# The last Mamba chunk of a convolution and attention network: one running sum in place of two, and the skip term on GpSimd

## The chip, the core and the metric

The kernel runs on one core of a Trainium2 chip. The metric is the device time of one execution in microseconds; of several runs the median is given. A core has five engines that run side by side, each with its own queue of instructions taken in order: TensorE (PE in the profile; its weight loads are the row PEld), VectorE (DVE), ScalarE (ACT), GpSimd (POOL) and SyncE (SP), which starts transfers. They meet through semaphores. TensorE writes its results into PSUM, from where VectorE and ScalarE read them; everything else lies in SBUF.

## What is computed

The network has four layers: a pair of Mamba blocks, a dynamic convolution, and two attention layers with mixtures of experts. The change concerns the second Mamba block of the first layer only:

```python
xs, res = jnp.split(u @ in_w + in_b, 2, axis=-1)
xs = silu(causal_conv(xs, conv_w) + conv_b)
dt, Bm, Cm = jnp.split(xs @ xproj_w, [DT_RANK, DT_RANK + D_STATE], axis=-1)
delta = softplus(dt @ dt_w + dt_b)
dA = exp(delta[..., None] * A)
dBu = delta[..., None] * Bm[:, :, None, :] * xs[..., None]
# scan over time: h = dA * h + dBu ; ys = sum over the 16 states of h * C
y = ys + xs * Dp
y = y * silu(res)
out = y @ out_w + out_b
# afterwards: x + layernorm(out)
```

There are 2 images of 1024 tokens, 256 channels, 512 inner channels and 16 states; all values are float32.

## The kernel before

A Mamba block (class `Mamba`) goes through its 2048 tokens in four chunks of 512 (`NCH`), and holds the inner channels as four groups of 128 partitions (`NDC`). A chunk has three parts. `front` makes xs, delta and du = delta times xs, and on GpSimd ends each of the four groups with the four operations of lines 405, 407, 409 and 411. `scan` runs over the 16 states n. For each of them GpSimd multiplies du by the broadcast row B in two halves of 128 x 1024 (line 461, tile `m_h`, six buffers), ScalarE makes exp(delta A) for each group (line 469, `m_da`), and VectorE runs the recurrence along the tokens (line 473). The states' outputs are then turned by TensorE so that tokens lie on partitions (line 440, `m_ht` in PSUM, three buffers), because C is then one number for each partition, and are multiplied by C and added to a running sum. This is the inner function `rest`, which is one state or more behind the recurrence. VectorE adds most of them into `ya` (line 449), but state 0 starts `ya` and state 10 (`ASIDE`) starts a second sum `yb`, each as an eviction by ScalarE (line 447).

`back` makes the gate: matmuls at line 496, evictions with bias at 500, Silu at 504. Then it turns both sums back to channels on partitions, and adds xs times D to them, all in one PSUM tile for each group. The skip is a product with a diagonal matrix (`skip`, line 517), and the sums are products with the identity (line 522). VectorE multiplies by the gate (526, in place of xs). Lines 534 and 538 form the output product, 545 the layer norm, 548 turns the result back, and for the last chunk 550 adds it into the residual `xt`, to which lines 510 to 513 have added the network's input and the norm's bias.

`layer0` strings this together as generators: while chunk u is scanned, `paced` advances the front of chunk u+1 and the back of chunk u-1 at given slots (first and end) of 63. In the last unit there is no next front. There `early()` runs in place of it, a part of the next layer's convolution for the first image (112 steps, line 795, tile `early_acc`), and the first seven steps of the chunk's own `back`: four gate groups, Silu, two residual additions. When the scan is over, `both` interleaves the rest of `back` with a last piece of that convolution, three convolution steps to one step of `back`. Then `layer1` begins. It loads the convolution's weights again (`pair`, line 773), turns the first image on POOL and PE (lines 889 and 890), and convolves the second image (line 795, tile `acc`), for which the last `xt` must be there.

The generators give the order in which the work is written. A scheduler decides the order in each engine's queue; an instruction can stand well before or after the slot at which it was written, but once the program is built, every queue is fixed. Tiles of one tag share buffers: the products of `back` and the gate use two PSUM buffers (tag `mm`).

Of the kernel before, what the change touches and what calls it, by code (L numbers as in the profile page):

```python
# [10 lines left out]
F32 = mybir.dt.float32  # L11
I32 = mybir.dt.int32
BF16 = mybir.dt.bfloat16
AF = mybir.ActivationFunctionType
# [5 lines left out]
P = 128  # L20
# [10 lines left out]
DI = 512  # L31
# [202 lines left out]
class Mamba:  # L234
# [177 lines left out]
            yield  # L412
        self.chunks[j] = xs, bd, ct, delta, du

    def scan(self, j, before, between, start=False):

        net, nc, m, scanp = self.net, self.net.nc, self.m, self.scanp
        xs, bd, ct, delta, du = self.chunks[j]
        state, first = self.state, self.first(j)
        ya = self.two.tile([P, TPC, DI], F32, tag="ya", name=f"{m}_ya_{j}")
        yb = self.one.tile([P, TPC, DI], F32, tag="yb", name=f"{m}_yb_{j}")
        self.chunks[j] = xs, ya, yb
        G = 2
        half = [P, G, TC]

        def keep(n, hs):  # L430
            for g, h in enumerate(hs):
                nc.scalar.copy(state[:, n, g * G : (g + 1) * G], h[:, :, TC - 1])

        def rest(n, hs):


            for i in range(TPC):
                ps = self.ps_ht.tile([P, DI], F32, tag="ht", name=f"{m}_ht_{j}_{n}_{i}")
                for dc in range(NDC):
                    nc.tensor.transpose(  # L440
                        ps[:, dc * P : (dc + 1) * P], hs[dc // G][:, dc % G, i * P : (i + 1) * P],
                        net.ident,
                    )
                yield
                c = ct[:, i, n : n + 1]
                if n in (0, self.ASIDE):
                    nc.scalar.activation((yb if n else ya)[:, i, :], ps, AF.Copy, scale=c)
                else:
                    nc.vector.scalar_tensor_tensor(  # L449
                        ya[:, i, :], ps, c, ya[:, i, :], ALU.mult, ALU.add  # L450
                    )
                if i == 0 and first:
                    keep(n, hs)

        for n in range(NS):
            b = scanp.tile([P, TC], F32, tag="b", name=f"{m}_b_{j}_{n}", bufs=4)
            nc.sync.dma_start(b, bd[n].partition_broadcast(P))
            hs = []
            for g in range(NDC // G):
                h = scanp.tile(half, F32, tag="h", name=f"{m}_h_{j}_{n}_{g}", bufs=6)  # L460
                made = (nc.vector if start and n == 0 else nc.gpsimd).tensor_mul(  # L461
                    h, du[:, g * G : (g + 1) * G, :], b.unsqueeze(1).to_broadcast(half)
                )
                hs.append(h)
            self.product = made
            for dc in range(NDC):
                da = self.ps_da.tile([P, TC], F32, tag="da", name=f"{m}_da_{j}_{n}_{dc}")
                i = dc * NS + n
                nc.scalar.activation(  # L469
                    da, delta[:, dc, :], AF.Exp, scale=self.aneg[:, i : i + 1]  # L470
                )
                h = hs[dc // G][:, dc % G, :]
                nc.vector.tensor_tensor_scan(  # L473
                    h, da, h, 0.0 if first else state[:, n, dc : dc + 1], ALU.mult, ALU.add
                )


                next(before, None)
                if n or dc:
                    next(between, None)  # L480
            before = chain(before, rest(n, hs))
        for _ in between:
            pass
        return before

    def back(self, j, last=False):


        net, nc, m, xt = self.net, self.net.nc, self.m, self.xt
        y, *sums = self.chunks.pop(j)  # L490
        tok = slice(j * TC, (j + 1) * TC)
        gate = self.one.tile([P, NDC, TC], F32, tag="gate", name=f"{m}_gate_{j}")
        for dc in range(NDC):
            ps = self.ps_mm.tile([P, TC], F32, tag="mm", name=f"{m}_g_{j}_{dc}")
            for kc in range(NCC):
                nc.tensor.matmul(  # L496
                    ps, lhsT=self.gate_sb[:, kc, dc * P : (dc + 1) * P], rhs=xt[:, kc, tok],
                    start=(kc == 0), stop=(kc == NCC - 1),
                )
            nc.scalar.activation(  # L500
                gate[:, dc, :], ps, AF.Identity, bias=net.col(f"{m}_in_b", NDC + dc)
            )
            yield
        nc.scalar.activation(gate, gate, AF.Silu)
        yield
        if last:
            for cc in range(NCC):
                x = self.one.tile([P, TC], F32, tag="r", name=f"{m}_x_{j}_{cc}", bufs=3)
                at = j % (HW // TC) * TC
                nc.sync.dma_start(x, self.x[j // (HW // TC), cc, :, at : at + TC])  # L510
                nc.gpsimd.tensor_scalar_add(x, x, net.col(f"{m}_ln_b", cc))
                nc.gpsimd.tensor_add(xt[:, cc, tok], xt[:, cc, tok], x)
                yield

        for dc in range(NDC):
            ps = self.ps_mm.tile([P, TC], F32, tag="mm", name=f"{m}_y_{j}_{dc}")
            nc.tensor.matmul(
                ps, lhsT=self.skip[:, dc, :], rhs=y[:, dc, :], start=True, stop=False
            )
            for k, ya in enumerate(sums):  # L520
                for i in range(TPC):
                    nc.tensor.matmul(
                        ps[:, i * P : (i + 1) * P], lhsT=ya[:, i, dc * P : (dc + 1) * P],
                        rhs=net.ident, start=False, stop=(k == 1 and i == TPC - 1),
                    )
            nc.vector.tensor_mul(y[:, dc, :], ps, gate[:, dc, :])
            yield
        o = self.one.tile([P, TPC, C], F32, tag="o", name=f"{m}_o_{j}")
        found = []
        for i in range(TPC):  # L530
            if i % 2 == 0:
                ps = self.ps_mm.tile([P, TC], F32, tag="mm", name=f"{m}_out_{j}_{i}")
            a = ps[:, i % 2 * C : (i % 2 + 1) * C]
            nc.tensor.matmul(
                a, lhsT=net.ones_row, rhs=self.out_b, start=True, stop=False
            )
            for dc in range(NDC):
                nc.tensor.matmul(
                    a, lhsT=y[:, dc, i * P : (i + 1) * P], rhs=self.out_sb[:, dc, :],
                    start=False, stop=(dc == NDC - 1),  # L540
                )
            found.append(a)
            yield
        tiles = [o[:, i, :] for i in range(TPC)]
        net.norm_rows(tiles, found, nc.scalar)
        yield
        for cc in range(NCC):
            ps = net.transposed(self.ps_mm, tiles, cc, "mm")
            if last:
                nc.vector.scalar_tensor_tensor(  # L550
                    xt[:, cc, tok], ps, net.col(f"{m}_ln_w", cc), xt[:, cc, tok],
                    ALU.mult, ALU.add,
                )
                yield
                continue
            r = self.one.tile([P, TC], F32, tag="r", name=f"{m}_r_{j}_{cc}", bufs=3)
            nc.scalar.activation(
                r, ps, AF.Identity, scale=net.col(f"{m}_ln_w", cc), bias=net.col(f"{m}_ln_b", cc)
            )
            nc.gpsimd.tensor_add(xt[:, cc, tok], xt[:, cc, tok], r)  # L560
            if self.x is not None:
                x = self.one.tile([P, TC], F32, tag="r", name=f"{m}_x_{j}_{cc}", bufs=3)
                at = j % (HW // TC) * TC
                nc.sync.dma_start(x, self.x[j // (HW // TC), cc, :, at : at + TC])
                nc.gpsimd.tensor_add(xt[:, cc, tok], xt[:, cc, tok], x)
            yield


def paced(n, parts):

    taken = [0] * len(parts)
    for slot in range(n):
        for i, (steps, many, first, end) in enumerate(parts):
            while taken[i] < many and slot >= first + (end - first) * taken[i] / many:
                next(steps, None)
                taken[i] += 1
        yield
    for steps, *_ in parts:
        for _ in steps:
            pass  # L580
# [11 lines left out]
def layer0(net, x, x_dram, m1, m2, load_image, taps, conv_dram, lg):  # L592
# [5 lines left out]
    with (  # L598
# [41 lines left out]
        for u, (m, j) in enumerate(units):  # L640
# [42 lines left out]
            own = m.back(j, u + 1 == len(units))  # L683
            if u + 1 == len(units):

                steps += [(islice(own, 7), 7, 44, 62)]
            before = m.scan(j, before, paced(63, steps), u == 0)
            done = [own]
        for _ in before:
            pass  # L690
# [1085 lines left out]
```

## Time and profile before

| what | us |
|---|---|
| three runs | 2169.64, 2165.42, 2167.72 |
| median | 2167.72 |
| profiled execution | 2167.17 |
| its span | 2165.4 |
| span up to the last chunk's first scan | 907 |
| from there to the first convolution matmul of layer 1 | 189 |
| from there to the end | 1069 |

| engine | busy us | share of the span |
|---|---|---|
| PE | 1890.4 | 87% |
| PEld | 1343.7 | 62% |
| DVE | 1403.3 | 65% |
| ACT | 957.8 | 44% |
| POOL | 1028.0 | 47% |

In the profile's lines a group reads: line of the kernel, engine, operation, tile written, tile read, partitions times elements, count. A note in brackets is the time for which the engine sat idle before that instruction, and what ended it. In the timeline the first number is the start in microseconds from the start of the span and the second the duration of the row. Rows of several instructions of one kind are merged (x8). The granted clock of TensorE is a share of full speed.

Around the last chunk the profile has these stages: the front of this chunk ends at about 904, the scan of its 16 states runs from 907 to 1048, the last addition into `ya` ends at 1061.5, the last convolution matmul of `early_acc` is at 1090, and `layer1`'s own convolution begins at 1096.4.

### The profile page before, as it was taken

To read this page: it belongs to the slowest core of one execution; us is meant where nothing else is said; L and a number is where in the kernel's file an instruction comes from. 1 tells how busy PE (TensorE), PEld (TensorE's weight loads), DVE (VectorE), ACT (ScalarE), POOL (GpSimd) and SP (SyncE) were. 2 spreads that over 40 slices of the span, in tenths; PEclk is the share of its full clock that TensorE was granted. 3 is DMA by queue.
4 is the path that set the end of the run, shared out by engine and by line. 5 is a ranking of instruction groups with operands and counts; after the bars stand their busy time and mean duration, and the time that the engine had idled before them with its cause. 6 is when DMAs were issued, how large, how long until landed. Compare 5 with 4: busy or idle time off the path is not lost.

```text
span 2165.4 us, 27316 instructions
## 1 busy us (share of the span) xinstructions
PE 1890.4 (87%) x9652; PEld 1343.7 (62%) x9652; DVE 1403.3 (65%) x2212; ACT 957.8 (44%) x1609; POOL 1028.0 (47%) x726
## 2 busy tenths in 40 slices
PE   6888899897989889799999899949999699859996
PEld 2364656555555555465655556639998467659994
DVE  6999999999999999897314575652222544432223
ACT  4677777767777767643213544311110132311011
POOL 3796788959697796964216410013332000023331
PEclk8969889798989979799999999969999799979997
DMA  3121121111112110310030100038998200069997
GB/s 107 45 69 40 37 65 41 59 33 54 54 48 61 38 51 31 87 38 25 10 55 1 49 15 10 20 121 299 328 327 305 83 10 10 20 221 325 331 327 286
DMA packets 90499, 223.87 MB, mean 103 GB/s; under 512 B 35467, under 2 KB 51728, under 8 KB 79732
## 3 DMA queue, kind: packets, MB, share of 16 engines
q1 hardware_dynamic: 77636, 198.29, 27.3%
q0 software_dynamic: 7728, 19.15, 2.9%
q10 hardware_dynamic: 4992, 4.59, 0.7%
q8 instruction: 81, 1.33, 0.3%
q14 instruction: 62, 0.51, 0.1%
HBM read 204.60 MB, written 19.37 MB: 103 GB/s over the span
## 4 chain that ended last, share of the span: by engine, by line
PE 30%; issue 17%; DVE 14%; POOL 10%; ACT 7%; DMA 4%; POOLq 0%; ACTq 0%; DVEq 0%
DVE m_h L473 7%; PE acc L795 3%; POOL x L1553 3%; POOL l_yd L1603 3%; DVE m_ya L449 3%; PE av L1309 3%; PE sc L1283 2%; DMA l_yd<-y,target 2%; PE early_acc L795 2%; PE h L1132 2%; PE m_ht L440 2%; ACT m_da L469 2%; POOL m_h L461 2%; PE w L1141 1%; DMA x<-l_zd,source 1%
## 5 line engine op out<-in xcount | busy, mean ns | idle before, releaser
L461 POOL TENSOR_TENSOR m_h<-m_du,m_b 128x1024 f32<-128x1024 f32 x254 | 594.4, 2363 | 223.4 <-PE m_ht L440 128.2
L440 PE MATMUL m_ht<-ident,m_h 128*128 128x128 f32 x2048 | 361.3, 308 | 105.3 <-DVE m_ya L449 76.2
L440 PEld LDWEIGHTS m_ht<-ident,m_h 128*128 128x128 f32 x2048 | 268.1, 157 | 297.2 <-issue 100.9
L469 ACT ACTIVATE m_da<-m_delta,m_aneg 128x512 f32<-128x512 f32 x512 | 348.9, 690 | 214.5 <-DVE m_h L473 214.0
L1553 POOL DMA_INDIRECT x<-l_zd,source x82 | 84.5, 1030 | 571.5 <-DVE source L1498 217.0
L449 DVE SCALAR_TENSOR_TENSOR m_ya<-m_ht,m_ct,m_ya 128x512 f32<-128x512 f32 x448 | 318.6, 731 | 31.1 <-PE m_ht L440 30.6
L473 DVE TENSOR_TENSOR_SCAN m_h<-m_da,m_state,m_h 128x512 f32<-128x512 f32 x256 | 316.8, 1267 | 29.2 <-POOL m_h L461 21.6
L473 DVE TENSOR_TENSOR_SCAN m_h<-m_da,m_h 128x512 f32<-128x512 f32 x256 | 302.7, 1207 | 18.0 <-ACT m_da L469 15.2
L1583 PEld LDWEIGHTS h<-xts,we 128*128 128x128 f32 x2528 | 297.4, 194 | 6.8 <-issue 3.1
L1583 PE MATMUL h<-xts,we 128*128 128x128 f32 x2528 | 298.5, 277 | 2.0 <-issue 1.5
L1590 DVE TENSOR_TENSOR hid<-hid,h 128x512 f32<-128x512 f32 x79 | 54.3, 687 | 256.1 <-PE h L1583 256.1
L1589 ACT ACTIVATE hid<-h 128x512 f32<-128x512 f32 x79 | 47.2, 597 | 381.6 <-PE h L1583 381.6
L1597 PE MATMUL o<-we,hid 128*128 128x256 f32 x632 | 150.4, 380 | 2.2 <-DVE y L1602 1.6
L1603 POOL DMA_INDIRECT l_yd<-y,target x79 | 79.0, 1000 | 142.6 <-DVE y L1602 137.9
L1597 PEld LDWEIGHTS o<-we,hid 128*128 128x128 f32 x632 | 113.7, 190 | 15.7 <-DVE y L1602 2.8
L336 PE MATMUL m_conv<-m_pre,m_taps 128*128 128x512 f32 x240 | 114.5, 596 | 6.1 <-ACT m_gate L500 5.6
L795 PE MATMUL early_acc<-x,early 128*98 128x448 f32 (+24 forms) x308 | 99.5, 449 | 0.0
L795 PE MATMUL acc<-x,pair 128*98 128x416 f32 (+21 forms) x308 | 94.1, 454 | 0.0
L1602 DVE COPY y<-o 128x256 f32<-128x256 f32 x79 | 33.5, 424 | 69.7 <-PE o L1597 69.7
L309 PE MATMUL m_in<-x,m_in_sb 128*128 128x512 f32 x128 | 67.3, 650 | 7.8 <-ACT m_pre L313 5.2
L496 PE MATMUL m_g<-x,m_gate_sb 128*128 128x512 f32 x128 | 69.9, 662 | 4.1 <-ACT m_o L168 2.1
L795 PEld LDWEIGHTS acc<-x,pair 128*98 128x98 f32 x308 | 48.0, 168 | 40.4 <-issue 35.0
(321 smaller groups left out, 2843.0 us busy)
## 6 DMA issues: line engine op xcount, KB each, us to landing
we<-in_l_experts_dram SPq DMA_DIRECT2D x82, 1536.0 KB, 9.4
m_b<-m_bd SPq DMA_DIRECT2D x128, 256.0 KB, 3.2
w<-in_l_w_dram SPq DMA_DIRECT2D x21, 256.0 KB, 3.9
l_zd<-l_z SPq DMA_DIRECT2D x7, 512.0 KB, 2.8
l_yl<-l_yd SPq DMA_DIRECT2D x10, 256.0 KB, 5.9
l_yl<-l_yd ACTq DMA_DIRECT2D x10, 256.0 KB, 5.9
early<-taps SPq DMA_DIRECT2D x7, 343.0 KB, 4.4
pair<-taps SPq DMA_DIRECT2D x7, 343.0 KB, 6.0
```

Of the source, the lines that this page charges most:

```text
L336: nc.tensor.matmul(ps, lhsT=self.taps[:, dc * 4 + k, :], rhs=pre[:, dc, k : k + TC], start=(k == 0), stop=(k == 3),)
L440: nc.tensor.transpose(ps[:, dc * P : (dc + 1) * P], hs[dc // G][:, dc % G, i * P : (i + 1) * P], net.ident,)
L449: nc.vector.scalar_tensor_tensor(ya[:, i, :], ps, c, ya[:, i, :], ALU.mult, ALU.add)
L461: made = (nc.vector if start and n == 0 else nc.gpsimd).tensor_mul(h, du[:, g * G : (g + 1) * G, :], b.unsqueeze(1).to_broadcast(half))
L469: nc.scalar.activation(da, delta[:, dc, :], AF.Exp, scale=self.aneg[:, i : i + 1])
L473: nc.vector.tensor_tensor_scan(h, da, h, 0.0 if first else state[:, n, dc : dc + 1], ALU.mult, ALU.add)
L496: nc.tensor.matmul(ps, lhsT=self.gate_sb[:, kc, dc * P : (dc + 1) * P], rhs=xt[:, kc, tok], start=(kc == 0), stop=(kc == NCC - 1),)
L795: nc.tensor.matmul(a[:, lo - 16 * k : hi - 16 * k, co : co + n], lhsT=lhsT, rhs=self.x[:, kc, b, lo - r0 : hi - r0, ci : ci + n], start=(u ...
L1553: nc.gpsimd.indirect_dma_start(out=x, out_offset=None, in_=zd[:, :], in_offset=bass.IndirectOffsetOnAxis(ap=source[:, g : g + 1], axis=0), ...
L1583: nc.tensor.matmul(ps[:, at], lhsT=w12[:, s, kc, at], rhs=xt[:, kc * P : (kc + 1) * P], start=(kc == 0), stop=(kc == NCC - 1),)
L1597: nc.tensor.matmul(ps[:, :C], lhsT=ht[:, mc * P : (mc + 1) * P], rhs=w[:, 8 + mc, :], start=(mc == 0), stop=(mc == NHC - 1),)
L1603: nc.gpsimd.indirect_dma_start(out=yd[g], out_offset=bass.IndirectOffsetOnAxis(ap=target[:, g : g + 1], axis=0), in_=y, in_offset=None, bo ...
```

## The change

For the last chunk alone there is no second sum: state 10 is added into `ya` by VectorE like the others. The skip is no longer a product of TensorE. GpSimd multiplies xs by D in place (four operations of 128 x 512, written for slots 6 to 40 of the scan), and after Silu multiplies this by the gate (four more, ahead of the residual additions). After the scan TensorE transposes `ya` only; VectorE multiplies the transpose by the gate and adds GpSimd's product, two operations for each group in place of one. The other chunks are as they were; the diagonal `skip` is still made for them.

```diff
-    def scan(self, j, before, between, start=False):
+    def scan(self, j, before, between, start=False, last=False):
...
-        yb = self.one.tile([P, TPC, DI], F32, tag="yb", name=f"{m}_yb_{j}")
-        self.chunks[j] = xs, ya, yb
+        sums = {0: ya}
+        if not last:
+            sums[self.ASIDE] = self.one.tile([P, TPC, DI], F32, tag="yb", name=f"{m}_yb_{j}")
+        self.chunks[j] = xs, *sums.values()
...
-                if n in (0, self.ASIDE):
-                    nc.scalar.activation((yb if n else ya)[:, i, :], ps, AF.Copy, scale=c)
+                if n in sums:
+                    nc.scalar.activation(sums[n][:, i, :], ps, AF.Copy, scale=c)
...
     def back(self, j, last=False):
...
+        if last:
+            for dc in range(NDC):
+                nc.gpsimd.tensor_scalar_mul(y[:, dc, :], y[:, dc, :], net.col(f"{m}_D", dc))
+                yield
         gate = self.one.tile([P, NDC, TC], F32, tag="gate", name=f"{m}_gate_{j}")
...
         nc.scalar.activation(gate, gate, AF.Silu)
         yield
         if last:
+            for dc in range(NDC):
+                nc.gpsimd.tensor_mul(y[:, dc, :], y[:, dc, :], gate[:, dc, :])
+                yield
...
             ps = self.ps_mm.tile([P, TC], F32, tag="mm", name=f"{m}_y_{j}_{dc}")
+            if last:
+                for i in range(TPC):
+                    nc.tensor.transpose(
+                        ps[:, i * P : (i + 1) * P], sums[0][:, i, dc * P : (dc + 1) * P], net.ident
+                    )
+                nc.vector.tensor_mul(gate[:, dc, :], ps, gate[:, dc, :])
+                nc.vector.tensor_add(y[:, dc, :], y[:, dc, :], gate[:, dc, :])
+                yield
+                continue
...
-                steps += [(islice(own, 7), 7, 44, 62)]
-            before = m.scan(j, before, paced(63, steps), u == 0)
+                steps += [(islice(own, 4), 4, 6, 40), (islice(own, 11), 11, 44, 62)]
+            before = m.scan(j, before, paced(63, steps), u == 0, u + 1 == len(units))
```

## The prediction

> **What bounds the kernel now.** I read the stretch in which the last chunk of Mamba is scanned and finished, 855 to 1100 us, because only that chunk's code changes. First the table by stage: which engine has no gap left.
>
> ```profile
> 905.00:920.00 15.00, 12.60 (x48) 6.73 (x47) 13.13 (x15) 7.56 (x14) 15.00 (x9) 0.83 0.51 120
> 920.00:935.00 15.00, 14.96 (x66) 8.87 (x67) 15.00 (x16) 8.47 (x13) 13.52 (x7) 1.00 0.27 67
> ...
> 1010.00:1025.00 15.00, 15.00 (x65) 9.32 (x64) 8.60 (x12) 6.32 (x8) 6.98 (x4) 1.00 0.00 0
> ...
> 1061.50:1071.00 9.50, 9.50 (x69) 7.92 (x67) 2.77 (x4) 0.00 (x0) 0.00 (x0) 1.00 0.01 2
> ```
>
> The columns are stretch, length, busy time of PE, PEld, DVE, ACT, POOL, then clock and DMA. The limit moves: GpSimd is full to 920, VectorE to about 964, TensorE from there to the end of the chunk (15.00 of 15, then 9.50 of 9.50). GpSimd looks half idle over the whole scan, but not where it begins. Second, the timeline of GpSimd there:
>
> ```profile
> 901.85 1.26 POOL L409 TENSOR_TENSOR m_delta<-m_delta,m_ln 128x512 f32<-128x512 f32 x1
> 903.19 1.26 POOL L411 TENSOR_TENSOR m_du<-m_delta,m_xs 128x512 f32<-128x512 f32 x1
> 904.41 4.66 POOL L461 TENSOR_TENSOR m_h<-m_du,m_b 128x1024 f32<-128x1024 f32 x2
> ...
> 916.24 16.25 POOL L461 TENSOR_TENSOR m_h<-m_du,m_b 128x1024 f32<-128x1024 f32 x7
> 933.96 4.67 POOL L461 TENSOR_TENSOR m_h<-m_du,m_b 128x1024 f32<-128x1024 f32 x2 [1.48 <-PE m_ht L440]
> ```
>
> From 855.75 to 932.5 no row has an idle note; the first one is at 933.96. Third, who waits for it, in the timeline of all engines:
>
> ```profile
> 903.14 0.69 ACT L500 ACTIVATE m_gate<-m_g,cols_sb 128x512 f32<-128x512 f32 x1 [6.55 <-POOL m_delta L409]
> ...
> 918.63 3.63 DVE L473 TENSOR_TENSOR_SCAN m_h<-m_da,m_state,m_h 128x512 f32<-128x512 f32 x3 [0.42 <-POOL m_h L461]
> ```
>
> VectorE waits for GpSimd's product at 918.63 and then has no pause over 0.1 us until 941.60. Fourth, the last two states of the scan, where TensorE is the limit:
>
> ```profile
> 1029.39 5.40 PE L496 MATMUL m_g<-x,m_gate_sb 128*128 128x512 f32 x8 [2.06 <-ACT m_o L168]
> ...
> 1039.71 4.68 POOL L461 TENSOR_TENSOR m_h<-m_du,m_b 128x1024 f32<-128x1024 f32 x2 [12.39 <-PE m_ht L440]
> ...
> 1045.13 1.27 DVE L473 TENSOR_TENSOR_SCAN m_h<-m_da,m_state,m_h 128x512 f32<-128x512 f32 x1
> ...
> 1046.32 0.72 DVE L449 SCALAR_TENSOR_TENSOR m_ya<-m_ht,m_ct,m_ya 128x512 f32<-128x512 f32 x1
> ...
> 1049.02 0.60 PE L440 MATMUL m_ht<-ident,m_h 128*128 128x128 f32 x4
> ```
>
> The two products of state 15 run back to back, and the second lies ready (1044.4) only 0.7 us before its scan at 1045.13. Fifth, the weight loads of TensorE in the tail, whose starts give its pace:
>
> ```profile
> 1063.67 0.97 PEld L522 LDWEIGHTS m_y<-ident,m_yb 128*128 128x128 f32 x8
> 1064.57 0.30 PEld L517 LDWEIGHTS m_y<-m_xs,m_skip 128*128 128x128 f32 x2
> 1065.11 0.19 PEld L522 LDWEIGHTS m_y<-ident,m_ya 128*128 128x128 f32 x1 [0.24 <-issue]
> ...
> 1066.32 0.97 PEld L522 LDWEIGHTS m_y<-ident,m_yb 128*128 128x128 f32 x8
> ...
> 1089.22 0.97 PEld L795 LDWEIGHTS early_acc<-x,early 128*98 128x98 f32 x10
> ```
>
> From one yb row to the next is 2.65 us for one quarter of y; the chain of waits has 0.86 of it for the skip and 1.78 for ya and yb together. Last, the price of the new GpSimd work, from single lines:
>
> ```profile
> L511 POOL TENSOR_SCALAR m_x<-m_x,cols_sb x2: 1562/1570/1578, 1047.5 to 1053.0; 128x512 f32<-128x512 f32 x2
> L409 POOL TENSOR_TENSOR m_delta<-m_delta,m_ln x28: 1262/1267/1282, 126.5 to 901.8; 128x512 f32<-128x512 f32 x28
> L409 DVE TENSOR_TENSOR m_delta<-m_delta,m_ln x4: 681/682/683, 43.8 to 50.1; 128x512 f32<-128x512 f32 x4
> ```
>
> **What the Trainium skill says.** GPSIMD Engine Reference, section 3.1 (Elementwise): a two-input operation takes about twice VectorE's time. The trace agrees: 1267 against 682 ns, 1.86 times. TensorE: Matmul & The Clock Gate, Part 1 (The HAM clock gate): after an idle window of about 3.4 us the array runs at half clock until a busy one has passed. The trace shows such a drop after a shorter pause: after the 2.06 us wait at 1029.39 eight matmuls took 5.40 us, where the pace of m_g at full clock (weight loads 0.43 apart from 1033.34) makes 3.44; 1.96 us were lost. Part 4 of that page (PE-mode transpose): transposes do not count as busy for that gate. No run here shows that alone.
>
> **The change part by part.** Besides durations I use the order in which the changed program holds each queue, which is fixed before it runs.
>
> 1. *y times D on GpSimd* (four tensor_scalar). Written for slots 6 to 40 of the scan, they nevertheless stand earlier: one behind each of the four L411 products of the last front, so three before the last L409 at 901.85 and the fourth before the first m_h of the last chunk at 904.41. That is the stretch without a gap. 4 x 1.57 = 6.3 us. Behind them wait the gate eviction on ScalarE (903.14, and with it the m_da behind it: +4.7) and all later m_h. State 0's products are ready 6.3 later, VectorE's scan at 918.63 starts at 924.9. From there it has no gap to take this up, and TensorE, which takes over as the limit at 964.14 out of a wait for VectorE's m_ya, begins its full stretch 6.3 later. Bounds: 4.7 if the fourth is hidden, 6.3 if all count. I take +6.3.
>
> 2. *State 10 added into ya by VectorE.* ScalarE loses four evictions of 0.68, and is not the limit (6.3 of 15 us busy). VectorE gains 4 x 0.73 = 2.9 us: one between the scans of state 12, three before those of state 13. Before 1012.78 VectorE stood idle 6.49 us waiting for m_h of state 13, which waits for the transposes of state 10; that hides all four. Cost 0; without that cover 2.9.
>
> 3. *y times gate on GpSimd* (four tensor_mul, 4 x 1.27 = 5.1 us). They stand between the two m_h of state 15. Silu ends at 1041.26, or 0.8 sooner since the last m_g moves ahead of an early-convolution matmul, so they wait for nothing: first product to 1042.05, gate products to 1047.1, second m_h to 1049.4, scan at 1049.45 in place of 1045.13. Behind that scan in VectorE's queue is the m_ya that started at 1046.32; it ends at 1051.4. It frees the PSUM buffer (three rotate) which m_ht at 1049.02 writes: TensorE waits until 1051.45, +2.4. That pause is longer than the one of 2.06, so I add its half-clock window, +1.9. Bounds: 0 (if the buffer is free) to 4.3. The eight x additions queued behind on GpSimd end near 1062 rather than 1055.95; L550 needs them only after 1080. On SP one residual load moves ahead of another; same cover.
>
> 4. *The tail.* Per quarter the four transposes that remain go at 0.11 each (rows of m_ht, eleven loads in 1.23), 0.44 in place of 2.65: 4 x 2.2 = 8.8 us less for TensorE. VectorE gets a second operation of 0.68 per quarter: eight at 0.66, 5.3 us in place of 2.8. In the changed order twelve early-convolution matmuls (24 records at 0.16, 3.9 us) stand among the transposes, while VectorE does these. With the last m_ya at 1061.46 as before: multiplications and additions 1062.35 to 1067.6, first output matmul 1065.75, held about 0.3 for the last additions, four outputs of 2.24 to 1074.85, the remaining 30 convolution matmuls 6.2 and three transposes 0.3 to 1081.45. The last such load ended at 1090.19 (the row at 1089.22): -8.7. Then the pair loads and the xs copies start that much sooner; the first acc load stood 6.2 after that point, and stays so. One xk pair moves behind it, +0.3. So -8.4; bounds -8.8 and -6.5 (VectorE's additions not covered).
>
> Sum: 6.3 + 0 + 2.4 + 1.9 - 8.4 = +2.2 us on the profiled execution, 2167.17 us (span 2165.4): 2169.4. The median of the three runs is 0.55 higher, which makes 2169.9. I say 2169.6.
>
> **The rivals.** *GpSimd's share is hidden* (12%): it is only 47% busy over the span, and half idle from 935 on. Then only the tail counts, 2167.7 - 8.4 = 2159.3. Against it stands the gapless stretch of the second view. *TensorE's clock* (18%), the slower side: taking matmuls out and leaving transposes and pauses lets the clock fall not once but three times, at m_ht of state 14, among the y transposes, and before the outputs, 1.9 each: 6.3 + 2.4 + 5.7 - 8.4 = +6.0, 2173.7; it decides from the third window. For it: 0.70 clock after one pause; against: in the old tail the clock stayed 1.00 through twelve transposes in a row. *VectorE's extra states are not covered* (6%): +2.2 + 2.9 = +5.1, 2172.8; the 6.49 us of idle time speak against it.
>
> **How the numbers follow.** Forecast 60%, other mishaps 4%. About 0.2%, 4.3 us, is what a measurement can tell from no change. The forecast reaches slower than that in 5 of its 60 parts and faster in none. GpSimd hidden gives 11 faster, 1 same; the clock 14 slower, 4 same; VectorE 4 slower, 2 same; the rest 2 and 2. Faster 0.11, same 0.64, slower 0.25. Range: low end 4.7 - 8.8 = -4.1, high end 6.3 + 4.3 - 6.5 + 0.3 = +4.4 plus the nearer part of the clock case, and 1 to 2 us for the scatter of a median (runs 2165.42 to 2169.64): 2162.5 to 2174.5.
>
> **What would show it.** Step 1: the scan that started at 918.63 starts near 925, and tensor_scalar rows of 1.57 lie among the L411 rows. Step 2: no new VectorE pause near state 13. Step 3: an idle note of about 2.4 us at m_ht for state 14, with a clock below 1 after it. Step 4: from the last m_ya to the last early-convolution matmul 20 us in place of 28.7. I am wrong if the scan is not late, or if the tail has idle TensorE time of over 1 us.

## The result, and the profile after

The changed kernel took 2171.99 us (median of 20 runs, 2167.02 to 2183.77) where the kernel before, on the same chip, took 2167.23 (20 runs): a ratio of 1.0026, 95% interval 1.0016 to 1.0036. A second timing gave 1.0020 (1.0009 to 1.0030; 2170.25 against 2166.68). It is slower by some 4 us (4.8 and 3.6 by these medians), which is just what can be told from no change.

The profile of the changed kernel is of one long execution, the longest of its 20:

```profile
core 0: 2182.1 us, clock 0.908
```

Its span is 16.7 us above that of the first profile of before, and only a small part of this belongs to the change. To see which, I paired each VectorE and TensorE instruction with the same one in the first profile of before and took how much later it starts. This execution is 8.9 us late at the place of 853 us, ahead of every changed instruction; 9.7 late at 1130, behind the region of the change; 16.6 late at the end. So the region costs +0.8. Within it the steps can be seen one by one.

First the timelines of ScalarE, GpSimd and VectorE in the changed kernel, where the last front ends and the last scan begins (start, duration, engine, line, operation; in brackets the idle time before and what ended it):

```profile
917.32 0.69 ACT L506 ACTIVATE m_gate<-m_g,cols_sb 128x512 f32<-128x512 f32 x1 [8.25 <-POOL m_delta L409]
917.36 1.26 POOL L411 TENSOR_TENSOR m_du<-m_delta,m_xs 128x512 f32<-128x512 f32 x1
918.73 1.57 POOL L496 TENSOR_SCALAR m_xs<-m_xs,cols_sb 128x512 f32<-128x512 f32 x1
920.26 4.67 POOL L463 TENSOR_TENSOR m_h<-m_du,m_b 128x1024 f32<-128x1024 f32 x2
...
934.51 3.63 DVE L475 TENSOR_TENSOR_SCAN m_h<-m_da,m_state,m_h 128x512 f32<-128x512 f32 x3 [0.42 <-POOL m_h L463]
...
949.84 2.36 POOL L463 TENSOR_TENSOR m_h<-m_du,m_b 128x1024 f32<-128x1024 f32 x1 [1.48 <-PE m_ht L442]
```

The scaling by D stands behind L411 and ahead of the first m_h of the last chunk. This is the fourth; the others lie behind the three earlier L411. The same scan that started at 918.63 before starts at 934.51: 15.9 later in an execution that was 8.9 late already, so 7.0 for the change. GpSimd's first idle note is still the 1.48 at m_ht, now at 949.84.

Second, the end of the scan, the timelines of GpSimd, VectorE and TensorE:

```profile
1053.90 2.36 POOL L463 TENSOR_TENSOR m_h<-m_du,m_b 128x1024 f32<-128x1024 f32 x1 [10.69 <-issue]
1056.21 4.96 POOL L514 TENSOR_TENSOR m_xs<-m_xs,m_gate 128x512 f32<-128x512 f32 x4
1061.13 2.35 POOL L463 TENSOR_TENSOR m_h<-m_du,m_b 128x1024 f32<-128x1024 f32 x1
...
1063.51 1.28 DVE L475 TENSOR_TENSOR_SCAN m_h<-m_da,m_state,m_h 128x512 f32<-128x512 f32 x1 [4.12 <-POOL m_h L463]
...
1065.58 1.09 PE L442 MATMUL m_ht<-ident,m_h 128*128 128x128 f32 x4 [2.22 <-DVE m_ya L451]
1066.46 2.89 PE L813 MATMUL early_acc<-x,early 128*98 128x448 f32 x4
```

The two m_h of state 15, back to back before, have the four gate products between them; VectorE waits 4.12 for the second, and TensorE 2.22 for the m_ya queued behind that scan. The transposes then take 1.09 where such a row took 0.60, and the next row 2.89 where it took 1.72 before: half clock, some 1.6 us.

Third, the tail, in the timeline of TensorE's weight loads:

```profile
1080.16 0.84 PEld L813 LDWEIGHTS early_acc<-x,early 128*98 128x98 f32 x6
1081.10 0.42 PEld L528 LDWEIGHTS m_y<-ident,m_ya 128*128 128x128 f32 x4
1081.49 0.27 PEld L813 LDWEIGHTS early_acc<-x,early 128*98 128x98 f32 x2
1081.76 0.51 PEld L528 LDWEIGHTS m_y<-ident,m_ya 128*128 128x128 f32 x4
...
1099.05 0.63 PEld L813 LDWEIGHTS early_acc<-x,early 128*98 128x98 f32 x6
```

A quarter of y takes 0.42 to 0.51 where it took 2.65. The last m_ya ends at 1079.64 and the last early-convolution load at 1099.68: 20.0 us, where it was 28.7. About one of these 8.7 us is lost again before the convolution of `layer1` begins: from that load to its first `acc` load it is 7.2 us, where it was 6.2.

### The profile page after: what moved, and what is told of

It is laid out like the page before. It is cut to its first block, busy times and chain, and to the rows that moved or that the text cites. A ratio compares the mean times of both kernels' runs of the same rounds, so it can differ in the third digit from the quotient of the medians.

```text
span 2182.1 us, 27219 instructions
## 1 busy us (share of the span) xinstructions
PE 1893.6 (87%) x9596; PEld 1344.5 (62%) x9596; DVE 1409.4 (65%) x2220; ACT 955.8 (44%) x1605; POOL 1040.5 (48%) x734
## 4 chain that ended last, share of the span: by engine, by line
PE 29%; issue 18%; DVE 13%; POOL 13%; ACT 6%; DMA 5%; POOLq 0%; ACTq 0%; SPq 0%; DVEq 0%
DVE m_h L475 6%; PE acc L813 3%; POOL x L1571 3%; POOL l_yd L1621 3%; DVE m_ya L451 3%; POOL m_h L463 3%; PE m_ht L442 3%; PE av L1327 3%; PE sc L1301 2%; DMA l_yd<-y,target 2%; PE h L1150 2%; PE early_acc L813 2%; ACT m_da L471 1%; PE w L1159 1%; DMA x<-l_zd,source 1%
## 5 line engine op out<-in xcount | busy, mean ns | idle before, releaser
L451 DVE SCALAR_TENSOR_TENSOR m_ya<-m_ht,m_ct,m_ya 128x512 f32<-128x512 f32 x452 | 323.0, 732 | 36.7 <-PE m_ht L442 35.0
```

The costliest lines, as they stand in the source:

```text
L451: nc.vector.scalar_tensor_tensor(ya[:, i, :], ps, c, ya[:, i, :], ALU.mult, ALU.add)
```

## The experiments

The shifts against the first profile of before, in us, as they build up between two places (times of that first profile). Each row is one profiled execution; rows with a figure at the end are repeats of the same kernel.

| profile | 853 to 920, D scalings | 1000 to 1040, m_g | 1040 to 1060, gate products | 1060 to 1097, tail | 1097 to 1130 | 1130 to the end |
|---|---|---|---|---|---|---|
| before_again | +2.4 | 0.0 | 0.0 | 0.0 | +0.1 | +2.6 |
| after | +7.0 | -1.7 | +4.0 | -7.6 | -0.9 | +6.9 |
| after_again | +6.6 | 0.0 | +2.4 | -7.6 | -0.6 | +3.4 |
| gate_late | +6.7 | 0.0 | 0.0 | -7.5 | -1.1 | +9.9 |
| d_held | 0.0 | 0.0 | +2.4 | -7.6 | -0.7 | +5.1 |
| d_held_2 | +0.4 | -1.7 | +2.4 | -7.6 | -0.4 | +1.5 |
| both_held | +0.1 | 0.0 | 0.0 | -7.5 | +0.5 | +3.2 |
| both_held_2 | +0.1 | -1.7 | 0.0 | -7.5 | -0.6 | +2.4 |
| both_held_3 | +0.7 | -1.7 | 0.0 | -7.5 | -1.1 | +7.0 |
| aside_only | 0.0 | 0.0 | 0.0 | -3.4 | 0.0 | +0.1 |
| aside_only_2 | +0.1 | 0.0 | 0.0 | -3.4 | -0.1 | +3.7 |
| aside_pad | +0.3 | -1.7 | 0.0 | -3.4 | -1.3 | +2.7 |
| skip_only | +0.1 | -1.7 | 0.0 | -2.8 | -0.3 | -0.1 |

And the times, the runs of each kernel's repeats taken together (differences of means; intervals are 1.96 standard errors, runs taken as independent; both_held_3, aside_only_2, aside_pad and skip_only ran on another chip, where the kernel before took 2167.4 in the mean, against 2167.0 and 2167.3 on the first):

| kernel | runs | mean us | mean granted clock | against before, us |
|---|---|---|---|---|
| before (beside the others) | 166 | 2167.2 | 0.9141 | |
| before_again | 23 | 2167.1 | 0.9137 | -0.1 +- 1.9 |
| after_again | 22 | 2171.3 | 0.9126 | +4.1 +- 1.3 |
| gate_late | 22 | 2172.0 | 0.9106 | +4.8 +- 1.8 |
| d_held, _2 | 36 | 2164.9 | 0.9129 | -2.4 +- 1.4 |
| both_held, _2, _3 | 39 | 2163.9 | 0.9117 | -3.4 +- 1.6 |
| aside_only, _2 | 28 | 2165.3 | 0.9140 | -1.9 +- 1.6 |
| aside_pad | 14 | 2165.4 | 0.9139 | -1.9 +- 1.8 |
| skip_only | 22 | 2163.2 | 0.9142 | -4.0 +- 1.6 |

**The same code again.** The changed kernel and the kernel before, unaltered.

> The changed kernel once more, unaltered, for the scatter of one execution. In its first profile the region of the change (from the first m_h of state 11 of the chunk before to the first acc matmul) is only 1.3 us longer than before, while 9.1 us were already lost ahead of it and 6.3 behind it, in code that the change does not touch. If those are scatter of single executions, this profile shows the same +1 to +2 in the region and other losses outside, within 3 us of the kernel before, and a time of 2169 to 2172. If the change slows the other stretches by something unseen (placement of buffers, order of transfers), the losses ahead of the region and behind it come back, 9 and 6 us.

> The kernel before, unaltered, against itself. It shows how far the same code drifts from one profiled execution to the next. In four of the five profiles of changed kernels so far, 1.2 to 2.9 us were lost against the first profile of the kernel before near 1270 and again near 1463 us, behind the region of the change. If these are scatter of TensorE's clock and of gather transfers, this profile shows shifts of the same size and either sign there, and a ratio within 0.1% of 1. If the changed kernels lose them because of the change, this profile agrees with the first within 0.5 us in both places.

The region of the change came out alike: after_again is 0.8 us longer from 853 to 1130, as the first profile was. What lies ahead of it is scatter: before_again, which is the kernel before, was 9.3 us late at 853, as late as the changed kernel's first profile (8.9), and 11.7 at 920. So the column from 853 to 920 can hold 2.4 us of scatter without any scaling in it; the other nine profiles without scalings there show 0.0 to 0.7. Its ratio to itself is 0.9995 (0.9985 to 1.0005). At the two places behind the region, near 1270 and 1463, before_again agreed with the first profile to 0.2 us. So what the changed kernels lose there was not shown to be scatter; more below.

**The scalings by D held back.** `behind` ties each step to the latest m_h product, so that the scheduler can't place it earlier.

```diff
-                steps += [(islice(own, 4), 4, 6, 40), (islice(own, 11), 11, 44, 62)]
+                steps += [(behind(m, islice(own, 4)), 4, 16, 40), (islice(own, 11), 11, 44, 62)]
```

> The four scalings by D are held behind the second m_h product of states 4, 5, 7 and 8 of the last chunk, so they leave the stretch in which GpSimd has no gap and run where it is half idle; everything else stands as in the changed kernel, and TensorE's order is the same. My theory (these four cost 6.3 us there and nothing later): 6.3 less than the changed kernel, 2165 to 2166 where that has 2172. Rival, GpSimd's share was hidden and the loss is elsewhere: no change, 2172. Rival, the half idle stretch is not free either because each scaling delays the next m_h by 1.57: only 0 to 3 less.

> The kernel with the scalings by D held back, once more, for its time and a second profile: 2163 to 2164. In the region of the change it lost 2.4 us at m_ht of state 14 in the first profile, at full clock. The half clock after that wait was seen in one of three profiles of kernels that have it; if it is a matter of chance it may be there or not in this one.

Ratios 0.9983 (0.9969 to 0.9996) and 0.9996 (0.9984 to 1.0008). Against after_again the mean is 6.5 us lower, with an interval of 1.7 either way. GpSimd's timeline of d_held:

```profile
913.87 16.23 POOL L463 TENSOR_TENSOR m_h<-m_du,m_b 128x1024 f32<-128x1024 f32 x7
930.09 1.57 POOL L496 TENSOR_SCALAR m_xs<-m_xs,cols_sb 128x512 f32<-128x512 f32 x1
931.62 4.65 POOL L463 TENSOR_TENSOR m_h<-m_du,m_b 128x1024 f32<-128x1024 f32 x2
936.26 1.55 POOL L496 TENSOR_SCALAR m_xs<-m_xs,cols_sb 128x512 f32<-128x512 f32 x1
939.62 4.67 POOL L463 TENSOR_TENSOR m_h<-m_du,m_b 128x1024 f32<-128x1024 f32 x2 [1.81 <-PE m_ht L442]
```

The same four instructions with the same 1.57 us cost nothing here: the second is followed by an idle time of 1.81, and the shift from 853 to 920 is 0.0 where the three profiles with the scalings in the front show 6.6 to 7.0. The rival that GpSimd's share was hidden falls; so does the one that each scaling delays the next m_h. Where they stand is the whole of their cost.

**The gate products behind the last m_h.**

```diff
-                steps += [(islice(own, 4), 4, 6, 40), (islice(own, 11), 11, 44, 62)]
+                steps += [(islice(own, 4), 4, 6, 40), (islice(own, 5), 5, 44, 52),
+                          (behind(m, islice(own, 4)), 4, 60, 63), (islice(own, 2), 2, 62, 63)]
```

> The four products by the gate come behind the second m_h product of state 15 instead of ahead of it. My theory: the 2.2 us wait of TensorE at m_ht of state 14 goes, and the half clock after it (1.7 us); 3.9 less than the changed kernel, 2168 where that has 2172. Rival, the clock falls anyway (at the y transposes or the outputs): only 2.2 less. Rival, the wait moves to the y stage because the gate products now end later (the first y result needs y times D times gate): no change or slower by 1 to 2.

GpSimd's and TensorE's timelines of gate_late:

```profile
1043.52 4.67 POOL L463 TENSOR_TENSOR m_h<-m_du,m_b 128x1024 f32<-128x1024 f32 x2 [12.39 <-PE m_ht L442]
1048.15 4.96 POOL L514 TENSOR_TENSOR m_xs<-m_xs,m_gate 128x512 f32<-128x512 f32 x4
...
1052.82 0.60 PE L442 MATMUL m_ht<-ident,m_h 128*128 128x128 f32 x4
```

The wait at m_ht is gone, and the shift from 1040 to 1060 with it, 2.4 us; the y stage did not wait instead (its tail is -7.5 like the others). But the time did not follow: 1.0026 (1.0014 to 1.0037), 0.7 us above after_again with an interval of 2.1, at a lower mean clock and with 9.9 us lost behind the region in the profiled execution.

**Both.**

```diff
+                steps += [(behind(m, islice(own, 4)), 4, 16, 40), (islice(own, 5), 5, 44, 52),
+                          (behind(m, islice(own, 4)), 4, 60, 63), (islice(own, 2), 2, 62, 63)]
```

> Both shifts at once: the scalings by D in the half idle stretch and the gate products behind the last m_h. My theory, the two losses lie one after the other on the path, so they add: 10.2 less than the changed kernel, 2161 to 2162, and 5 to 6 less than the kernel before. Rival, taking away the first only lets TensorE reach another limit (the transposes and early-convolution matmuls fill its time from 964 on): 4 less than the changed kernel, 2168, no better than before.

> Both shifts once more. In its first profile the region of the change is 2.4 us shorter than with the scalings alone held back, yet the median is 2.4 higher, at a mean granted clock of 0.9111 against 0.9134. If that was scatter: 2161 to 2163, 1 to 3 below the kernel with one shift, at the same clock. If putting the gate products last costs something outside the region, the median is again 1 to 3 above it, and the clock again 0.002 lower.

> The kernel with both shifts a third time, to pool its time: 2161 to 2165, and over the three timings 2 to 5 us below the kernel before. In the region of the change 7 us shorter than before, 2.4 of them by the gate products behind the last m_h.

Ratios 0.9994 (0.9979 to 1.0009), 0.9983 (0.9967 to 0.9999) and 0.9982 (0.9967 to 0.9997). The three together are 3.4 us below before and 1.0 below d_held, the latter with an interval of 2.0. In the region both steps add as expected: 7.0 to 9.7 shorter than before in all three profiles. In the time I expected 5 to 6 less than before and saw 3.4.

**The two halves of the change alone.** In aside_only the last chunk has no second sum, and the skip term stays on TensorE, so GpSimd has nothing new:

```diff
+        sums = {0: ya}
+        if not last:
+            sums[self.ASIDE] = self.one.tile([P, TPC, DI], F32, tag="yb", name=f"{m}_yb_{j}")
...
-                        rhs=net.ident, start=False, stop=(k == 1 and i == TPC - 1),
+                        rhs=net.ident, start=False, stop=(k == len(sums) - 1 and i == TPC - 1),
```

> The kernel before with one half of the change: the last chunk keeps no state aside (state 10 is added into ya by VectorE), while the skip term stays on TensorE and GpSimd gets nothing new. TensorE's order is that of before less the sixteen yb products. My theory: four times 0.89, 3.6 us less, 2163 where the kernel before has 2166.7, with no new pause of VectorE near state 13. Rival, VectorE's four additions (2.9 us) are not covered: 0.7 less, 2166. Rival, the tail is bound by something other than TensorE: no change.

> The kernel without the state aside, and with the skip term still on TensorE, once more. In its first profile the region of the change was 3.4 us shorter than before and the stretch from 1130 to 1500 as long as before (+0.3); in all seven profiles of kernels that have the skip term on GpSimd that stretch was 1.3 to 8.6 us longer, 4.2 in the mean. If that follows the moved skip term, this profile again shows less than 1 there, and the two timings together lie 2 to 3.5 below before. If it is chance, this profile can show 1 to 4 there as well.

The tail is 3.4 us shorter in both profiles, for 3.6 expected, and nothing was lost from 960 to 1040, where VectorE has the four more additions. Its weight loads:

```profile
1058.84 0.30 PEld L519 LDWEIGHTS m_y<-m_xs,m_skip 128*128 128x128 f32 x2
...
1060.59 0.30 PEld L519 LDWEIGHTS m_y<-m_xs,m_skip 128*128 128x128 f32 x2
```

One quarter takes 1.75 in place of 2.65. The time fell by 1.9 (ratios 0.9994, 0.9978 to 1.0010, and 0.9989, 0.9977 to 1.0001), less than 3.4 but with an interval that reaches it.

In skip_only the skip term is on GpSimd, placed as in both_held, and the second sum stays; the y stage adds the two sums by identity products:

```diff
-        if not last:
+        if True:
...
+                    for k, ya in enumerate(sums):
+                        nc.tensor.matmul(
+                            ps[:, i * P : (i + 1) * P], lhsT=ya[:, i, dc * P : (dc + 1) * P],
+                            rhs=net.ident, start=(k == 0), stop=(k == 1),
+                        )
```

> The other half of the change: the skip term by GpSimd, with both its steps held back as in the kernel with both shifts, while state 10 is still kept aside and TensorE adds ya and yb by identity products. TensorE saves 0.86 a quarter, 3.4 us, and VectorE has two operations of 0.66 a quarter; in this order no early-convolution matmuls stand among the y products, so the first output waits for VectorE, some 1.5 to 2. I expect the region of the change 1.5 us shorter than before, with an idle time of TensorE before the first output of 1 us or more. Rival, VectorE keeps up: 3.4 shorter. If the moved skip term makes the stretch from 1130 to 1500 longer, it does so here too (1.3 or more).

Here I was wrong: TensorE's timeline of skip_only has no idle note before the first output.

```profile
1065.49 0.39 PE L529 MATMUL m_y<-ident,m_yb 128*128 128x128 f32 x2
1065.72 0.49 PE L815 MATMUL early_acc<-x,early 128*98 128x192 f32 x2
1066.13 0.69 PE L554 MATMUL m_out<-rows_m_out_b,ones_row 1*128 1x256 f32 x2
```

A quarter's eight identity products take 1.79 (eight steps of 0.22 between rows), longer than VectorE's two operations (1.3), so VectorE keeps up as the rival had it; the tail is 2.8 shorter, and the ratio 0.9981 (0.9971 to 0.9992). The two halves sum to 6.2 of the 7.5 of the whole. Only in the whole do transposes at 0.11 take the place of summed identity products at 0.22, sixteen times, which is 1.8; that is more than the missing 1.3, but about one us of the whole's gain is lost again ahead of `acc`. The sum was not closed further.

**Dead work on GpSimd.** To see whether the loss behind the region comes from the shifted instruction stream of GpSimd alone, aside_only got eight small memsets in the half idle stretch.

```diff
+                def pad():
+                    for _ in range(8):
+                        nc.gpsimd.memset(net.small.tile([P, 4], F32, tag="ln_rs", name="pad"), 0.0)
+                        yield
+                steps += [(behind(m, pad()), 8, 16, 40)]
```

> The same kernel plus eight memsets of 128x4 on GpSimd, held behind the m_h products of states 4 to 10 of the last chunk: dead work of some 0.1 us each in the half idle stretch, so that GpSimd's program has as many more instructions as the changed kernel's, with none of its work. Theory that the loss from 1130 to 1500 comes from the shift of GpSimd's program (where its instructions are fetched, when its gathers are issued): 1.3 us or more longer there. Theory that it comes from the moved work or from chance in the gathers: less than 1 there, and the time of the kernel without the memsets.

From 1130 to 1500 this profile lost 2.6 us, most of it (1.9) near 1250 to 1280 and only 0.2 at 1463. The time of the 14 runs is that of aside_only (0.9989, 0.9977 to 1.0001). So the count of GpSimd's instructions does not bring the loss at 1463; what the 1.9 follows comes in the last section.

**What is lost behind the region.** The places can be named. Before and after in TensorE's timeline, first in the kernel before:

```profile
1257.51 1.88 PE L1085 MATMUL q<-zt,wq_sb 128*128 128x512 f32 x4
...
1463.70 0.41 PE L1567 MATMUL xt<-ident,x 128*128 128x128 f32 x2 [1.94 <-DMA x<-l_zd,source]
```

And in the changed kernel:

```profile
1268.57 2.69 PE L1103 MATMUL q<-zt,wq_sb 128*128 128x512 f32 x4
...
1477.04 0.42 PE L1585 MATMUL xt<-ident,x 128*128 128x128 f32 x2 [3.33 <-DMA x<-l_zd,source]
```

The same four matmuls at less than full clock, and a gather for the experts that lands later while the experts' weights are being loaded. From 1130 to 1500 the eight profiles that have both halves of the change lost 1.3 to 8.6 us, 4.3 in the mean; before_again, aside_only (twice), skip_only and aside_pad lost 0.1, 0.3, 0.0, -0.3 and 2.6. The two places are of different kinds.

Near 1270 six profiles lost 1.9 us and all others at most 0.2. The six are five of the eight, and aside_pad; so this loss doesn't follow the change. It follows the clock's grid, as the last section shows.

At the gather near 1463 the loss follows the change without exception. The eight lost 0.8 to 3.6 us there, the other five at most 0.2, and TensorE waited 3.06 to 4.09 for that gather, where it waited 1.87 to 2.23 in the others and in the kernel before. What comes in between is seen among the transfers. In the changed kernel GpSimd issues this gather at 1469.1, and before it lands, at 1471.9, a packet of 16 KB is moved that carries instructions; in the view of the DMA queues from 1470 to 1474:

```profile
q8 instruction: 1, 0.02, 1.6%
```

In all eight profiles such a packet falls about 3 us behind the issue of the gather and takes 1.0 to 1.1 us. In the other six, the kernel before among them, the nearest packets of this queue lie over 12 us ahead of the issue, and over 6 us behind the landing. The kernel before has 81 of them, one for every 243 of TensorE's matmuls and loads in the trace, and their spacing is steadiest when counted in TensorE's instructions (a relative spread of 0.23, against 0.6 to 0.8 in those of the other engines). So I take them for TensorE's program. State 10 alone takes 64 instructions from TensorE's queue, the skip term as in skip_only 16, and the whole 112; with the dead work on GpSimd it is 64, as without it. In times of the first profile the packet moves from 1440.0 to about 1444, to 1440.3, and to about 1460 accordingly, and only the last lies in the gather (issued at 1457.0). That it delays the gather agrees with all 14 profiles, but no run moved the packet by itself: the cause is likely, not shown.

## Why the prediction was right or wrong

The forecast of 2169.6 was 2.4 us under the median, with the time inside the range of 2162.5 to 2174.5. Its likeliest case, a change within 0.2%, stands at the edge: 0.26%, and 0.20% at the second timing, both with intervals that reach below 0.2%. The change itself was forecast as +2 us and is about twice that. By its steps:

1. *y times D: right.* Forecast +6.3, measured 6.6 to 7.0 in three profiles, and 6.5 +- 1.7 in the time when it was taken away. Three of the reasons held: the four stand in the front although they are written for slots 6 to 40, the stretch has no gap, and VectorE doesn't catch up (the shift is constant from 920 to 1000).
2. *State 10 in VectorE: right.* Forecast 0; from 960 to 1030 no profile gains or loses more than 0.1.
3. *y times gate: the wait right, the clock over-sized.* Forecast 2.4 for the wait: measured 2.22 as a note and 2.4 as a shift in four of four profiles, and 0.0 when the products go last. The half-clock window, +1.9, I added as certain: it came in one of the four (the 4.0 in the row of after, 1.6 above the others). The mean is 0.4. The loss after the pause at m_g, from which I took the 1.9, is 1.7: the same eight matmuls that took 5.40 take 3.70 in aside_pad, where the clock stays.
4. *The tail: right.* Forecast -8.4 with the start of acc; measured 8.7 us less up to TensorE's last convolution load, as forecast. The start of `acc` did not keep its distance of 6.2 behind it, so that up to 1097 -7.5 to -7.6 are left in all eight profiles with both halves of the change, and another +0.5 to -1.1 (-0.6 in the mean) come up to 1130.

So within the region the forecast was +2.2 and the measured value +0.8 in both profiles of the changed kernel: the 1.9 for the clock was too much by 1.5 in the mean. That the two profiles agree is luck: the first paid for the half clock at m_ht (1.6) and was spared the one at m_g (1.7), the second the other way round.

5. *What the sum doesn't have.* It ends at the start of `acc` and carries its +2.2 unchanged to the end of the kernel: what lies behind was taken to cost the same, without a reason. In the two profiles of the changed kernel it cost 6.9 and 3.4 more, 5.3 and 3.7 of it up to 1500; before_again lost 0.1 up to 1500 and 2.6 up to the end. Region and rest together are 7.8 and 4.3, beside the 4.1 to 4.8 of the times. At the gather it is the longer wait, 2.9 and 1.3 us with what follows it; near 1270 it is half clock, 1.9 in both. So the forecast came as near as it did because two errors have opposite signs: the region was forecast 1.4 too long, and the rest was left out.

A run's time also goes with its mean clock: within a kernel, 0.001 less goes with about 1 us more, and the changed kernel ran at 0.9126 against 0.9141. But the kernel with both shifts ran at 0.9117 and was faster than before, so this is not a cause that stands by itself.

Of the rivals, *GpSimd's share is hidden* is shown false by d_held. *VectorE's extra states are not covered* is shown false by aside_only. *TensorE's clock* (2173.7) is not what happened either: the clock did not fall among the y transposes or before the outputs. That its time, and that of VectorE's extra states (2172.8), lie nearer to the measured 2171.99 than the forecast is luck.

The kernels with one or both shifts show the same as the change itself: the region's gain arrives in the time less 3 us or more. Taking away the wait at m_ht shortened the region by 2.4 in every profile, and the time by only 0.2 (mean of gate_late against after_again and both_held against d_held), interval 1.4 either way. That the wait costs its 2.4 us in the time was thus not shown.

## What to carry to other kernels

An engine that is half idle over a stage can be full where the stage begins. Four operations that cost nothing in the idle stretch cost 6.5 us in the full one, and a slot in the source didn't keep them out of it; an explicit dependence on a later instruction did. With the gate products held back as well the kernel is 0.16% below the one before; the skip term alone, held back in the same way, gives as much (4.0 us against 3.4, which the intervals don't tell apart). Read the final order of each queue before pricing an "idle" engine. And where a change is worth a few us in two thousand, add up the shifts by stage over several profiles: single executions of the same code differed by 9.3 us before the change was reached. A stage that the change does not touch can move too: here a gather some 370 us later.

## What the runs showed of the hardware that I had not expected

The granted clock follows a grid. In the trace's record of it every stretch at one clock lasts a multiple of 3.413 us (3413, 6827, 10240 ns and so on), but for the last one, and where the grid lies differs from one execution to the next. So one and the same pause may or may not be followed by half clock. The wait of 2.06 us ahead of m_g led to 3.4 us at half clock in 8 of 14 profiles, and the other six gained 1.7 us there (the column of m_g; the profile of after is one of them). Laid beside the grid, this is not chance: in the eight the pause between the matmuls (2.87 us) lies wholly within one step of the grid, in the six a step ends inside it. The loss near 1270 goes the same way: the pause of 2.0 us before the last mm_t there lies within one step in the six profiles with the loss, and across two in the eight without. The rule is not complete: a pause of 2.05 us some 5 us earlier, at kvt, lies within one step in seven profiles, and no half clock follows. The wait of 2.2 at m_ht reaches across two steps in all four profiles that have it, and led to half clock in 1 of 4, the one with 2.8 of its 2.9 us in one step (at most 2.5 in the others). The rows of m_g behind the pause took 5.40 with the half clock (the kernel before); in aside_pad, without it:

```profile
1032.18 3.70 PE L498 MATMUL m_g<-x,m_gate_sb 128*128 128x512 f32 x8 [2.06 <-ACT m_o L168]
```

In after_again, TensorE's timeline, the wait is the same as in the changed kernel's first profile, and the rows behind it are at full clock:

```profile
1056.42 0.63 PE L442 MATMUL m_ht<-ident,m_h 128*128 128x128 f32 x4 [2.21 <-DVE m_ya L451]
1056.88 1.72 PE L813 MATMUL early_acc<-x,early 128*98 128x448 f32 x4
```

The Trainium skill, TensorE: Matmul & The Clock Gate, Part 1 (The HAM clock gate), says that the activity window is free-running, and that the count of slow matmuls therefore varies from run to run of one kernel. These traces agree, with 3.413 us for the window. I had read its idle window of about 3.4 us as a threshold and then put the drop after 2.06 us down as a rule; priced as a chance, a pause of 2.2 us here is worth 0.4 to 1 us besides its length. The time at half clock in one execution was 335 to 386 us over the 14 profiles (without the last stretch), and a run's time goes with its mean clock (correlation -0.6 to -0.8 within a kernel): a good part of the scatter between runs.
